# The output layer's statistics, normalisation and first transpositions move into the last chunk of the last graph layer

## The chip, the cores and the metric

The kernel runs on one core of a Trainium2 chip. Its time is the device time of one execution in microseconds; the figure for the kernel before is the median of three runs. Five engines work side by side, each with a queue of its own: TensorE (PE, with PEld for its weight loads), VectorE (DVE), ScalarE (ACT), GpSimd (POOL) and SyncE (SP), which issues most of the DMAs.

## The reference, cut to what matters

A network of four layers works on N = 2708 nodes with D = 256 features in float32. Each layer is a graph attention followed by a feed-forward part, both with a residual. Only the last layer and a helper of the third are touched:

```python
# layer 3, the last
x = x + elu(softmax(where(adj > 0, leaky_relu(f1[:, None] + f2[None, :]), NEG), axis=1) @ Wh)
#   with h = layernorm(x), Wh = h @ W, f1 = Wh @ a1, f2 = Wh @ a2
x = x + (layernorm(x) @ weight.T + bias)          # the output layer
```

The output layer needs, for each row of x, its mean and variance over the 256 features, so a row can only be normalised when the attention of that row is complete. Rows don't depend on each other in this layer.

## The kernel before, in words

The nodes are 22 tiles of 128 rows, the last one with 20 (`NT = 22`, `LAST = 21`). `X` holds all of x in SBUF, one slice `X[:, t, :]` per tile, through the whole kernel. A planner that knows the engines orders each engine's instructions when the program is built: it takes them in the order of the text where it can, and lets an engine take later ones while an earlier one waits. `issue_after(x)` keeps instructions behind x, and `manual_schedule(engines={PE})` gives TensorE the order of the text, with no moves.

The attention of one head is `gat_single` (L1301); the third graph layer runs it with the key g2 (plain residual), the fourth with g3 (`elu` true). After a projection stage it goes through the rows to be computed in chunks of `W = 6 * P` columns: three chunks of six tiles (0 to 5, 6 to 11, 12 to 17) and a last one of three (18 to 20). Tile 21, with its 20 rows, is done apart, in `tail_sums`. In each chunk, j runs over the 22 tiles of neighbours:

- `gat_pairs` (L721) makes `e`: L731 on ScalarE (an activation), L732 on VectorE (times the mask). `e` has three buffers.
- L1463 adds `e` times `V` to one accumulator `acc` per tile of the chunk. A chunk of six tiles is six matmuls per j, the last chunk three. Each float32 matmul leaves two records in the profile.

The accumulators come from a pool of eight PSUM banks. After a chunk, for each tile: L1469 `rd` (VectorE, reciprocal of the sum), L1477 `h` (ScalarE, scaled copy, which frees the bank), then the ELU and residual: L1479 `g` = min(h, 0), L1480 exp on ScalarE, L1481 `h` = max(h, 0) - 1, L1482 and L1483 additions, the last into `X`. One tile's run of L1479 to L1483 is called a unit below. `rd` has two buffers, `h` six.

`tail_sums` (L81) does tile 21 at the start of the last chunk: L87, 22 narrow matmuls into one bank; L89, a ScalarE copy `ts`; L91, one matmul that folds it into a second bank.

The output layer is `linear_ffn` (L2427), called after everything of g3 is closed. It opens its own pools (PSUM: three buffers each of `tp` and `po`), loads the weights `w` (256 KB) and the bias `b` over POOL's queue, and takes statistics in groups of four tiles (`ln_stats`, L112: L160 and L161 on VectorE, L163 a Sqrt on ScalarE, L167 a reciprocal). Exp and Sqrt need different tables of ScalarE, each change being a row `ACT_TABLE_LOAD`. Then per tile:

- L124 `f` = (X - mean) * rstd on VectorE
- L132, two transpositions on TensorE into `tp`; L2443, the copy `ft` on ScalarE
- L2444, X + b on POOL
- L139, two matmuls into `po` (four records of the profile); L2448 `o` = po + X on VectorE; L2449, the store on SP. `o` has three buffers.

Of the kernel before, what the change touches and what calls it, by code (L numbers as in the profile page):

```python
# [52 lines left out]
class Net:  # L53
# [27 lines left out]
    def tail_sums(self, pool, work, et, V):  # L81
# [8 lines left out]
        ps = pool.tile([P, D + 1], F32, name="acc")  # L90
        nc.tensor.matmul(ps[: rows(LAST)], self.quarter[:, : rows(LAST)], ts, start=True, stop=True)  # L91
        return ps
# [81 lines left out]
def cosine_gnn(net, ctx, kept, x_in):  # L174
# [7 lines left out]
    with ExitStack() as ctx:  # L182
# [101 lines left out]
        for n, (i0, iw) in enumerate(chunks(512)):  # L284
# [25 lines left out]
            if len(whole) < len(its):  # L310
                with tc.issue_after(ended.ins):
                    acc.append(net.tail_sums(ptail, work, et, F))
# [988 lines left out]
def gat_single(net, key, head, feed, elu):  # L1301
# [7 lines left out]
    with ExitStack() as ctx:  # L1309
# [120 lines left out]
        work = ctx.enter_context(tc.tile_pool(name=f"{key}work", bufs=3))  # L1430
        pacc = ctx.enter_context(tc.tile_pool(name=f"{key}acc", bufs=8, space=PSUM))
# [9 lines left out]
        nc.vector.scalar_tensor_tensor(ev, ev, 1.0, net.mask[:, :, whole:], ALU.max, ALU.mult)  # L1441
        for i0 in range(0, whole, W):
            iw = min(W, whole - i0)
            its = tiles_of(i0, iw)
            acc = [pacc.tile([P, D + 1], F32, name="acc") for _ in its]
            if i0 + iw == whole:
                acc.append(net.tail_sums(pacc, work, et, V))
            for j in range(NT):
# [12 lines left out]
                for k, i in enumerate(its):  # L1461
                    ri = rows(i)
                    nc.tensor.matmul(  # L1463
                        acc[k][:ri], e[:, k * P : k * P + ri], V[:, j, :], start=j == 0, stop=j == NT - 1
                    )
            for k, i in enumerate([*its, LAST][: len(acc)]):
                r = rows(i)
                rd = small.tile([P, 1], F32, name="rd")
                nc.vector.reciprocal(rd[:r], acc[k][:r, D : D + 1])  # L1469
                if not elu:  # L1470
# [7 lines left out]
                g = work.tile([P, D], F32, name="g")  # L1478
                nc.vector.tensor_scalar(g[:r], h[:r], 0.0, None, ALU.min)  # L1479
                nc.scalar.activation(g[:r], g[:r], AF.Exp)  # L1480
                nc.vector.tensor_scalar(h[:r], h[:r], 0.0, -1.0, ALU.max, ALU.add)  # L1481
                nc.vector.tensor_tensor(g[:r], g[:r], h[:r], ALU.add)  # L1482
                nc.vector.tensor_tensor(X[:r, i, :], X[:r, i, :], g[:r], ALU.add)  # L1483
# [924 lines left out]
def biased_gnn(net, head, route):  # L2408
# [3 lines left out]
    gat_single(net, "g2", head, results, False)  # L2412


def elu_gnn(net, kept, head, route):
# [8 lines left out]
    gat_single(net, "g3", head, results, True)  # L2424


def linear_ffn(net, out):  # L2427

    nc, tc, a, X = net.nc, net.tc, net.a, net.X
    with ExitStack() as ctx:  # L2430
        big = ctx.enter_context(tc.tile_pool(name="f3big", bufs=1))
        work = ctx.enter_context(tc.tile_pool(name="f3work", bufs=3))
        psum = ctx.enter_context(tc.tile_pool(name="f3p", bufs=3, space=PSUM))
        w = net.load_weight(big, a["f3_wT"], "w")
        b = net.load_rows(big, a["f3_b"], D, "b")
        ln = net.ln_stats()
        for t in range(NT):
            r = rows(t)
            f = work.tile([P, D], F32, name="f")
            net.normed(f, t, ln)  # L2440
            ps = net.transposed(psum, f, r)
            ft = work.tile([P, 2, P], F32, name="ft")
            nc.scalar.copy(ft[:, :, :r], ps[:, :, :r])  # L2443
            nc.gpsimd.tensor_tensor(X[:r, t, :], X[:r, t, :], b[:r], ALU.add)  # L2444
            po = psum.tile([P, D], F32, name="po")
            net.matmul_k(po[:r], ft[:, :, :r], w)
            o = work.tile([P, D], F32, name="o")
            nc.vector.tensor_tensor(o[:r], po[:r], X[:r, t, :], ALU.add)  # L2448
            nc.sync.dma_start(out[span(t), :], o[:r])  # L2449
# [148 lines left out]
```

## Time and profile before

| | |
|---|---|
| median of three runs | 2592.28 us (2589.53 to 2594.91) |
| the profiled execution | 2596.85 us, span 2595.1 us |
| TensorE busy over the span | 2422.7 us, 93% |
| VectorE, ScalarE, POOL busy | 1464.5, 1058.4, 358.2 us |
| last chunk and tail sums, 2524.60 to 2557.40: TensorE, VectorE, ScalarE busy | 32.27, 21.61, 20.23 of 32.80 us |
| output layer, 2557.40 to 2592.30: TensorE, VectorE, ScalarE, POOL busy | 29.04, 24.90, 12.20, 14.39 of 34.90 us |
| granted TensorE clock, whole span | 0.966 |

A row of the timeline gives the start in us from the span's start, the length, engine, line and operation, the tiles written and read, their size, how many instructions are merged, and in brackets how long the engine had been idle and what ended that. The windows give busy time per engine with the number of instructions, then the granted clock of TensorE (1.00 is full speed), the share of DMA and GB/s.

### The profile page before, as it was taken

How to read it: one execution, taken by the hardware profiler on the slowest of the kernel's cores; microseconds unless marked ns; L12 is line 12 of the kernel's file. 1: busy time of each engine (PE TensorE's matmuls, PEld its weight loads, DVE VectorE, ACT ScalarE, POOL GpSimd, SP SyncE). 2: the span in 40 equal slices, each digit the busy share in tenths (PEclk: the TensorE clock that was granted, in tenths of full speed). 3: DMA queues.
4: the chain of work that ended last, by engine and by line, in shares of the span. 5: the costliest groups of instructions: out<-in, count | busy, mean ns of one | idle time of the engine just before them, and what ended most of it. 6: DMA issues, size and time to landing. Idle time of an engine off the chain costs nothing. (4 is left out here: it accounts for less than half of the span.)

```text
span 2595.1 us, 32725 instructions
## 1 busy us (share of the span) xinstructions
PE 2422.7 (93%) x11708; PEld 1576.9 (61%) x11708; DVE 1464.5 (56%) x3331; ACT 1058.4 (41%) x1698; POOL 358.2 (14%) x470
## 2 busy tenths in 40 slices
PE   5899998999999999979799989999979999979998
PEld 4666765686333334458678864434447777757887
DVE  7753437746888876333544557877843222243556
ACT  3444453214877773321344333344422222234454
POOL 1000003100000001134230011222232222210002
PEclk9999999979999999989899999999989999989999
DMA  8899512000000003664220010000342222150001
GB/s 286 289 290 350 176 49 71 1 6 1 1 1 1 1 1 91 168 182 157 83 74 1 1 33 25 28 25 25 112 132 52 33 34 33 22 172 1 1 1 44
DMA packets 113178, 198.00 MB, mean 76 GB/s; under 512 B 8898, under 2 KB 72128, under 8 KB 110178
## 3 DMA queue, kind: packets, MB, share of 16 engines
q1 hardware_dynamic: 90856, 149.82, 18.1%
q0 software_dynamic: 18736, 41.56, 6.3%
q10 hardware_dynamic: 3422, 4.46, 0.6%
q8 instruction: 99, 1.62, 0.3%
q14 instruction: 65, 0.53, 0.1%
HBM read 132.97 MB, written 62.83 MB: 75 GB/s over the span
## 5 line engine op out<-in xcount | busy, mean ns | idle before, releaser
L732 DVE SCALAR_TENSOR_TENSOR e<-e,mask 128x768 f32<-128x768 f32 (+3 forms) x352 | 417.6, 1217 | 244.8 <-ACT e L731 242.3
L731 ACT ACTIVATE e<-big_p,minus_one,ratio 128x768 f32<-128x768 f32 (+3 forms) x352 | 418.6, 1226 | 284.1 <-PE acc L1463 195.0
L1463 PE MATMUL acc<-V,e 128*128 128x257 f32 x1848 | 403.6, 381 | 5.6 <-DVE e L732 5.5
L1463 PEld LDWEIGHTS acc<-V,e 128*128 128x128 f32 x1848 | 351.5, 190 | 58.0 <-issue 6.9
L2274 PE MATMUL h<-w,ft 128*128 (+1 forms) x752 | 234.8, 454 | 0.5 <-ACT ft L2256 0.5
L307 PE MATMUL acc<-F,e 128*128 128x257 f32 (+1 forms) x924 | 212.5, 383 | 3.9 <-DVE e L303 3.5
L928 PE MATMUL acc<-e,V 128*64 128x512 f32 (+1 forms) x1056 | 209.7, 550 | 1.3 <-DVE e L732 1.3
L307 PEld LDWEIGHTS acc<-F,e 128*128 128x128 f32 (+1 forms) x924 | 171.6, 189 | 56.8 <-DVE e L303 29.4
L2291 DVE TENSOR_TENSOR hh<-hh,h 128x682 f32<-128x682 f32 x47 | 40.7, 866 | 240.7 <-PE h L2274 240.7
L2274 PEld LDWEIGHTS h<-w,ft 128*128 128x128 f32 x752 | 135.8, 191 | 56.3 <-issue 1.8
L928 PEld LDWEIGHTS acc<-e,V 128*64 128x64 f32 x1056 | 73.9, 138 | 151.6 <-issue 145.9
L303 DVE TENSOR_TENSOR e<-e,mask 128x512 f32<-128x512 f32 (+2 forms) x132 | 80.5, 621 | 141.0 <-ACT e L296 139.3
L2061 ACT ACTIVATE e<-sc 128x1024 f32<-128x1024 f32 (+4 forms) x131 | 107.4, 862 | 114.6 <-PE sc L2052 90.3
L2083 DVE TENSOR_TENSOR sum<-sum,e 128x1024 f32<-128x1024 f32 (+4 forms) x131 | 136.8, 1045 | 21.3 <-PE po L2077 11.2
L296 ACT ACTIVATE e<-score 128x512 f32<-128x512 f32 (+2 forms) x132 | 69.5, 544 | 170.4 <-PE score L294 145.4
L2306 PE MATMUL po<-w,ht 114*128 (+1 forms) x564 | 129.7, 379 | 0.9 <-DVE ht L2299 0.9
L2052 PE MATMUL sc<-qt,kt 64*128 64x512 f32 (+5 forms) x568 | 121.6, 546 | 1.4 <-ACT sum L2061 0.9
L2306 PEld LDWEIGHTS po<-w,ht 114*128 114x128 f32 x564 | 106.5, 189 | 22.6 <-DVE ht L2299 8.2
L939 PE MATMUL den<-e,low 128*3 128x512 f32 (+1 forms) x1056 | 117.7, 542 | 0.0
L294 PE MATMUL score<-QK 128*128 128x512 f32 (+2 forms) x264 | 111.9, 552 | 3.4 <-ACT e L296 3.0
L2077 PE MATMUL po<-e,V 128*64 128x512 f32 (+5 forms) x524 | 107.5, 527 | 1.9 <-DVE e L2067 1.9
L1869 POOL DMA_INDIRECT dys<-y,to x47 | 73.7, 1569 | 208.1 <-ACT ft L2256 190.8
(645 smaller groups left out, 3357.7 us busy)
## 6 DMA issues: line engine op xcount, KB each, us to landing
row<-in_adj SPq DMA_DIRECT2D x21, 1354.0 KB
raw<-in_adjT SPq DMA_DIRECT2D x35, 768.0 KB
hs<-zero SPq DMA_DIRECT2D x8, 2860.0 KB
hidden<-hr SPq DMA_DIRECT2D x32, 256.0 KB
wd<-in_f_wd SPq DMA_DIRECT2D x8, 1024.0 KB
kept<-mask SPq DMA_DIRECT2D x21, 338.5 KB
mask<-kept SPq DMA_DIRECT2D x21, 338.5 KB
w<-in_d_w1T SPq DMA_DIRECT2D x8, 682.0 KB
```

What stands on the lines that cost most here:

```text
L294: nc.tensor.matmul(ps[:r, :iw], QK[:, 0, span(j)], QK[:, 1, i0 : i0 + iw], start=True, stop=True)
L307: ended = nc.tensor.matmul(acc[k], e[:r, k * P : (k + 1) * P], F[:r, j, :], start=j == 0, stop=j == NT - 1)
L731: nc.scalar.activation(v, big_p[:, i], AF.Relu, bias=net.minus_one, scale=ratio)
L732: return nc.vector.scalar_tensor_tensor(v, v, 1.0, net.mask[:, j, i], ALU.add, ALU.mult)
L928: nc.tensor.matmul(acc[n][half, :iw], V[:, j, h, :], e[n][:, k, :iw], start=j == 0, stop=j == NT - 1)
L939: nc.tensor.matmul(den[g : g + Q, :iw], low[:, j, h, Q - 1 - q : 2 * Q - 1 - q], e[n][:, k, :iw], start=False, stop=j == NT - 1 and q == Q ...
L1463: nc.tensor.matmul(acc[k][:ri], e[:, k * P : k * P + ri], V[:, j, :], start=j == 0, stop=j == NT - 1)
L2052: nc.tensor.matmul(by_pairs(ps[:r, g], m, iw)[:, :, o:], kt[b, span(j)], qt[b, :, o:iw], start=True, stop=True)
L2077: nc.tensor.matmul(by_pairs(outs[n, p][b], m, iw)[:, :, o:], V[:r, j, g, :], by_pairs(e[:r, g], m, iw)[:, :, o:], start=j == 0, stop=j == ...
L2083: nc.vector.tensor_tensor(total, total, by_heads(e[:r], m, iw)[:, :, :, o:], ALU.add)
L2274: last = nc.tensor.matmul(halves[s, n][:, q, :HALF], fts[s][:, c, :], weights.w13[n][:, es[s], c, q * HALF : (q + 1) * HALF], start=c == 0 ...
L2306: last = nc.tensor.matmul(po, ht[:KP, k, :], w2[:KP, es[s], k, :], start=k == 0, stop=k == KC - 1)
```

## The change

- `tail_sums` returns a function `added` for its last matmul, the fold. `gat_single`, for g2 as for g3, calls it after j = 2 of the last chunk; the first graph layer calls it at once.
- `linear_ffn` becomes a class `Linear`, which g3 gets as `tail`. Its pools are opened inside g3, before the pool of accumulators, and `w` and `b` loaded there. It has no PSUM pool of its own and takes banks from the accumulators' pool.
- At a chunk's end only `rd` (now six buffers) and `h` are issued. The units of a chunk follow in the next chunk, one at each odd j behind the mask.
- `Linear.step` runs behind the mask of each j: statistics of the six tiles of the chunk before, one tile at j = 4, 6, ... 14; at j = 16 the inverse root of all six by Newton's method on VectorE (`inverse_root`, 12 small instructions) in place of Sqrt; from j = 16 one normalisation per j (L124's operation) with its addition of the bias on POOL. In the last chunk also the transpositions of tiles 0 and 1, at j = 18 and 20. `f` has 18 buffers, `ft` four.
- In the last chunk of g3 and after it TensorE's order is that of the text. `Linear.finish` then goes through the tiles: for t, the transpositions of t + 2, and the matmuls, `o` and store of t. The statistics of tiles 18 to 21, with the one Sqrt that is left, come in at t = 4.

```diff
@@ tail_sums
-        ps = pool.tile([P, D + 1], F32, name="acc")
-        nc.tensor.matmul(ps[: rows(LAST)], self.quarter[:, : rows(LAST)], ts, start=True, stop=True)
-        return ps
+
+        def added():
+            ps = pool.tile([P, D + 1], F32, name="acc")
+            nc.tensor.matmul(ps[: rows(LAST)], self.quarter[:, : rows(LAST)], ts, start=True, stop=True)
+            return ps
+
+        return added
@@ gat_single
+        hs = []
+
+        def unit(i, h):
+            r = rows(i)
+            g = work.tile([P, D], F32, name="g")
+            nc.vector.tensor_scalar(g[:r], h[:r], 0.0, None, ALU.min)
+            nc.scalar.activation(g[:r], g[:r], AF.Exp)
+            nc.vector.tensor_scalar(h[:r], h[:r], 0.0, -1.0, ALU.max, ALU.add)
+            nc.vector.tensor_tensor(g[:r], g[:r], h[:r], ALU.add)
+            nc.vector.tensor_tensor(X[:r, i, :], X[:r, i, :], g[:r], ALU.add)
+
         for i0 in range(0, whole, W):
             iw = min(W, whole - i0)
             its = tiles_of(i0, iw)
+            ending = tail and i0 + iw == whole
+            if ending:
+                ctx.enter_context(tc.manual_schedule(engines={mybir.EngineType.PE}))
+            if i0 + iw == whole:
+                added = net.tail_sums(pacc, work, et, V)
             acc = [pacc.tile([P, D + 1], F32, name="acc") for _ in its]
-            if i0 + iw == whole:
-                acc.append(net.tail_sums(pacc, work, et, V))
             for j in range(NT):
...
+                if j == 2 and i0 + iw == whole:
+                    acc.append(added())
+                if tail:
+                    with tc.issue_after(masked.ins):
+                        if hs and j % 2:
+                            unit(*hs.pop(0))
+                        tail.step(its[0], j, ending, pacc)
             for k, i in enumerate([*its, LAST][: len(acc)]):
                 r = rows(i)
-                rd = small.tile([P, 1], F32, name="rd")
+                rd = small.tile([P, 1], F32, name="rd", bufs=6)
...
                 nc.scalar.activation(h[:r], acc[k][:r, :D], AF.Copy, scale=rd[:r])
-                g = work.tile([P, D], F32, name="g")
...
+                hs.append((i, h))
+            while ending and hs:
+                unit(*hs.pop(0))
+            if ending:
+                tail.finish(pacc)
@@ in place of linear_ffn
+class Linear:
...
+    def norm(self, t):
+        r, X = rows(t), self.net.X
+        self.fs[t] = self.work.tile([P, D], F32, name="f", bufs=18)
+        self.net.normed(self.fs[t], t, (self.ln.mean, self.ln.rstd))
+        self.net.nc.gpsimd.tensor_tensor(X[:r, t, :], X[:r, t, :], self.b[:r], ALU.add)
+
+    def step(self, t0, j, ending, psum):
+
+        k, m = divmod(j - 4, 2)
+        if t0 and m == 0 and 0 <= k < 6:
+            self.ln.sums(t0 - 6 + k, t0 - 5 + k, root=False)
+        if t0 and j == 16:
+            self.ln.newton(self.work, t0 - 6, t0)
+            self.known = t0
+        if len(self.fs) < self.known:
+            self.norm(len(self.fs))
+        if ending and j in (NT - 4, NT - 2):
+            self.turned(len(self.fts), psum)
+
+    def turned(self, t, psum):
+        net, r, f = self.net, rows(t), self.fs[t]
+        ps = psum.tile([P, D + 1], F32, name="acc")[:, :D].rearrange("p (c m) -> p c m", c=2)
+        for c in range(2):
+            net.nc.tensor.transpose(ps[:, c, :r], f[:r, c * P : (c + 1) * P], net.ident[:r, :r])
+        ft = self.fts[t] = self.work.tile([P, 2, P], F32, name="ft", bufs=4)
+        net.nc.scalar.copy(ft[:, :, :r], ps[:, :, :r])
+
+    def result(self, t, psum):
+        net, nc, r = self.net, self.net.nc, rows(t)
+        po = psum.tile([P, D + 1], F32, name="acc")[:, :D]
+        net.matmul_k(po[:r], self.fts[t][:, :, :r], self.w)
+        o = self.work.tile([P, D], F32, name="o")
+        nc.vector.tensor_tensor(o[:r], po[:r], net.X[:r, t, :], ALU.add)
+        nc.sync.dma_start(self.out[span(t), :], o[:r])
+
+    def finish(self, psum):
+
+        early = self.known
         for t in range(NT):
-            net.normed(f, t, ln)
-            ps = net.transposed(psum, f, r)
...
+            if t == 4:
+                self.ln.sums(early, NT)
+                self.ln.roots(early, NT)
+            if t + 2 < NT:
+                if t + 2 not in self.fs:
+                    self.norm(t + 2)
+                self.turned(t + 2, psum)
+            self.result(t, psum)
```

## The prediction

> **What bounds the kernel now.** I read the page first, for the bound of the whole: TensorE is busy 93% of the span, and the chain that ended last closes with the output layer's matmuls.
>
> ```profile
> span 2595.1 us, 32725 instructions
> PE 2422.7 (93%) x11708; PEld 1576.9 (61%) x11708; DVE 1464.5 (56%) x3331; ACT 1058.4 (41%) x1698; POOL 358.2 (14%) x470
> ...
> PE po L139 1%; PE tp L132 0%; ACT ft L2443 0%; DVE f L124 0%; DVE o L2448 0%; ACT h L1477 0%; ACTq L2443 0%; DVE rstd L167 0%; DVEq L2448 0%
> ```
>
> Then the timeline of TensorE over the last 80 us, which is where the diff works. Columns: start, length, engine and line, count, and in brackets the idle time before and what ended it.
>
> ```profile
> 2524.64 2.79 PE L87 MATMUL acc<-V,et 128*32 128x257 f32 x44
> 2527.96 0.61 PE L91 MATMUL acc<-ts,quarter 128*20 128x257 f32 x2 [0.53 <-ACT ts L89]
> 2528.50 28.90 PE L1463 MATMUL acc<-V,e 128*128 128x257 f32 x132
> 2560.48 1.54 PE L132 MATMUL tp<-ident,f 128*128 128x128 f32 x6 [3.08 <-ACT h L1477]
> 2561.82 5.04 PE L139 MATMUL po<-w,ft 128*128 128x256 f32 x12
> 2567.86 0.41 PE L132 MATMUL tp<-ident,f 128*128 128x128 f32 x2 [1.00 <-DVE f L124]
> 2568.81 0.41 PE L132 MATMUL tp<-ident,f 128*128 128x128 f32 x2 [0.54 <-DVE f L124]
> 2569.05 1.89 PE L139 MATMUL po<-w,ft 128*128 128x256 f32 x8
> ...
> 2574.38 0.82 PE L132 MATMUL tp<-ident,f 128*128 128x128 f32 x6
> 2575.28 2.86 PE L139 MATMUL po<-w,ft 128*128 128x256 f32 x12
> ...
> 2589.64 2.10 PE L139 MATMUL po<-w,ft 128*128 128x256 f32 x8 [0.29 <-ACT ft L2443]
> ```
>
> The last chunk is solid TensorE work until 2557.40. The output layer then takes 34.44 us, until the last o starts on VectorE at 2591.84, with four kinds of loss: 3.08 us before the first transposition (its PSUM banks belong to a pool that opens when the last h copy has released the old one), 1.00 and 0.54 us for f (rows 2567.86, 2568.81), a wait for ft after every three tiles, and a slow first group (x12 takes 5.04 us; later ones 2.86). The last is the clock: the same stretch cut in windows, with the granted clock in the third column from the end.
>
> ```profile
> 2556.10:2559.50 3.40, 1.30 (x6) 0.78 (x5) 1.96 (x10) 2.70 (x5) 1.51 (x3) 1.00 0.00 0
> 2559.50:2562.90 3.40, 2.42 (x9) 2.11 (x10) 3.02 (x11) 2.48 (x9) 0.00 (x0) 0.50 0.00 0
> 2562.90:2566.30 3.40, 3.40 (x10) 2.69 (x9) 2.93 (x12) 1.65 (x3) 0.00 (x0) 0.50 0.11 39
> ```
>
> TensorE was busy 1.30 of 3.40 us, and the next 6.8 us ran at half clock. The Trainium skill (TensorE: Matmul & The Clock Gate, Part 1) has the gate close after an idle window of about 3.4 us; here 3.08 us sufficed, so I treat a busy share, not a full idle window, as the trigger.
>
> **The output layer after its move.** The built order shows TensorE's queue after the last accumulation as tp(t+2), po(t) for t = 0 to 19, then po(20), po(21): 20 pairs of transpositions and 22 pairs of matmuls. Two pairs of transpositions went into the chunk, behind j = 18 and j = 20. Prices: a po tile is four records; the x8 row starts at 2569.05 and its successor at 2570.78, so 0.216 each, 0.864 per tile. Six transpositions take 0.82 us of which 0.27 is the last one's latency: 0.109 each, 0.218 per tile. If nothing waits, 22 x 0.864 + 20 x 0.218 = 23.4 us, plus 0.1 to VectorE: the last o starts 23.5 us after the last accumulation, instead of 34.44. Gain 10.9 us. It is made of the 3.08 us, about 3 us of half clock, 1.9 us of waits for f, some 2.4 us of waits for ft, and 0.44 us of transpositions put in the chunk.
>
> Does anything wait? Walked by hand over the three queues from the last accumulation (T = 0):
> - Of the eight banks, tp(2) and po(0) get ones that are free long before, tp(4) and po(2) those of tiles 18 and 19, whose h copies end by 0.5 us; later a bank is free once its ft or o has been read out.
> - ScalarE does h(18), h(19), one exp, h(20), h(21), one exp, and only then ft(2): at 0.36 to 0.47 us each it ends near 2.3 us, and po(2) is due at 2.4. This is the tightest place; I put 0.1 us of wait inside the stall below. Then ft(3) ends at 3.0, due 3.5, and the margin grows to over 1 us.
> - VectorE does the last four tiles' units, then o(0) at about 4.1 us, and has caught up with the matmuls by o(7). The one Sqrt table load (1.28 us on ScalarE) falls after ft(8), and ft(9) still ends 1 us before it is due; f(18) is ready near 9.6 us, and its transposition is due at 17.7.
> - Output: in the trace's DMA packets the first o, begun at 2564.14, had landed by 2565.90, 1.76 us. With three o buffers that permits one tile in 0.6 us; TensorE gives one in 1.08.
>
> **The fold of the tail sums.** L91 waited for the ScalarE copy ts: from the end of L87 (2527.43) to the first accumulation (2528.50) is 1.07 us, of which L91 itself needs 0.43. After the change nine accumulations stand between, so 0.64 us is gained. The third graph layer has the same edit and the same row (L87 ends at 1488.96, accumulations begin at 1489.98): 0.59 us. Copies h issued ahead of all units at a chunk's end take away a 0.34 us pause at 2412 where a bank waited for an h: 0.3. Together 1.5 us.
>
> **What the last chunk pays.** Four transpositions: 0.44 us of TensorE. Statistics, Newton's inverse root and normalisation of tiles 0 to 11 go into earlier chunks with 2.6 us per j, of which VectorE uses 0.96: hidden. In the last chunk a j has 1.30 us. VectorE issues: mask 0.48; a unit 0.20 + 0.20 + 0.34 + 0.34 = 1.07 on odd j from 1 to 11; statistics 0.42 on even j from 4 to 14. So two j cost 0.95 + 1.07 + 0.42 = 2.44 of 2.60 us: hidden with little to spare. With three e buffers, e(j) can be masked 1.14 us before it is needed, and this is the cover. From j = 16 it doesn't reach. Newton is 12 small dependent operations (0.164 each in the table of groups, 0.22 with the hand-over): 2.7 us. Then come five normalisations before the last mask, and each starts a bias addition on POOL, which shows here:
>
> ```profile
> 1322.91 2.88 DVE L732 SCALAR_TENSOR_TENSOR e<-e,mask 128x768 f32<-128x768 f32 x2
> ...
> 1341.67 0.96 DVE L732 SCALAR_TENSOR_TENSOR e<-e,mask 128x768 f32<-128x768 f32 x1 [1.26 <-ACT e L731]
> ...
> 2567.31 0.40 DVE L124 TENSOR_SCALAR f<-X,mv,rstd 128x256 f32<-128x256 f32 x1
> 2567.76 2.69 DVE L124 TENSOR_SCALAR f<-X,mv,rstd 128x256 f32<-128x256 f32 x4
> ```
>
> The first row lies under POOL's additions of a bias in the third layer, the second after them: a mask is stretched from 0.96 to 1.4 us. A normalisation goes from 0.33 us per issue to 0.73. By these rows: 2.7 + 0.33 + 4 x 0.73 + 5 masks x 0.48 + 3 x 0.26 of stretch = 9.1 us, against 5 x 1.30 + 0.44 + 1.14 = 8.1 us: TensorE waits 1.0 us. The skill speaks harder against the change: SBUF — State Buffer, "Who interferes with whom", has whoever comes second blocked for the whole of the other's instruction. Then each of five normalisations or masks loses a POOL addition of 0.77 us: 2.7 + 5 x 0.33 + 2.4 + 5 x 0.77 = 10.6, and TensorE waits 2.5 us. I take the rows, 1.0 us; the ends are 0 (no contention: 6.75 us) and 2.5. Behind a late mask, in the fixed TensorE order, stand the transpositions and everything else of TensorE.
>
> POOL and SP issue the same instructions in the same order as before: weights (256 KB) and bias go out behind the mask's flags at the start of the layer, and POOL stands idle 245.21 us before the first addition. The weights now wait for the projection stage's buffers; only the bias and the additions queue behind them. No cost.
>
> **Sum.** 10.9 + 1.5 - 0.44 - 1.0 = 11.0 us. The profiled execution took 2596.85 us, 1.75 more than its span, and becomes 2585.9. It lies 4.6 us above the median of the runs; on the median 2592.28 the same 11.0 us gives 2581.3 us, 0.42% faster. The runs before spread from 2589.53 to 2594.91, so about 0.2%, 5.2 us, is what a measurement tells from no change.
>
> **Rivals.**
> - The last chunk stalls enough to lose the clock. The 2.5 us wait of the harsher reading leaves a 3.4 us window poorly filled, and 6.8 us at half clock follow (as above): 1.5 + 3.4 us less gain, 6.1 us, 2586.2 us. For it: the stretched rows and 0.73 us of measured stretch per normalisation; against: by the rows the excess is 1 us, under a third of a window.
> - Writing out is the bound. The steady groups before wrote three tiles in 3.59 us. If that is already the rate of the writes (1.2 us a tile), 22 tiles take 26.3, 2.9 us less gain: 2584.2 us. Against it: 1.76 us of landing with three buffers, and higher rates elsewhere on the page.
> - The lookahead fails, and it gets slower. Each po waits for its own ft: transposition 0.22, latency 0.16, copy 0.37, two hand-overs 0.1, matmuls 0.864 with 0.1 for an unprefetched weight load, 1.81 us a tile, 39.9 for 22. The loss against 34.44 is 5.4 us, and 1.0 + 0.44 - 1.5 leaves it there: 2597.6 us. It decides from (34.44 - 23.5) / 22 = 0.50 us of wait in each tile. For it: a wait for ft after each group before, and a fixed order that lets nothing pass. Against: ft has four buffers, and each transposition stands two tiles ahead.
> - It doesn't do what it says, because the end of the kernel is set elsewhere. The chain ends in po and o, so this needs a bound I don't see: 2592 us.
>
> **How the numbers follow.** Main 0.70; lost clock 0.17; writes 0.05; lookahead failing 0.04; no effect 0.04. The first three are faster by over 0.2%: 0.92, less 0.01 for a lost clock that costs more; same 0.05; slower 0.04. The range: below, no stall (1.0) and 2 us for the spread of a median, 2578; above, the lost clock's 2586.2 and 1.3 for the spread, 2587.5. What lies beyond is the last two cases and some of the second.
>
> **What would show it.** The first L132 transposition outside the chunk within 0.3 us of the last accumulation; no half clock between there and the end; one po tile in about 1.08 us, and some 23.5 us from the last accumulation to the last o; no wait for ts before the fold; masks from j = 17 on the ones TensorE waits for, about 1 us in all. The prediction is wrong if po waits for ft in each tile, if o waits for a DMA, or if masks from j = 3 to 15 come late.

## The result, and the profile after

| | before | after |
|---|---|---|
| median of 12 runs each | 2593.37 us (2589.53 to 2599.89) | 2583.55 us (2577.48 to 2589.30) |
| ratio, with its 95% interval | | 0.9956 [0.9946, 0.9967] |
| the profiled execution, its span | 2596.85, 2595.1 us | 2585.36, 2583.2 us |
| last accumulation to the start of the last o | 34.44 us | 23.81 us |
| first L87 to the end of the last accumulation | 32.76 us | 33.22 us |

The kernel is faster by 0.44%; the interval means 8.6 to 14.0 us. The prediction said 2581.3 us, 11.0 us less than before; the medians differ by 9.8 us, the spans by 11.9.

The page of the kernel after gives these busy times. Over the span TensorE has as many instructions as before and 2 us less busy time.

```profile
PE 2420.7 (94%) x11708; PEld 1575.7 (61%) x11708; DVE 1472.5 (57%) x3362; ACT 1050.1 (41%) x1687; POOL 360.8 (14%) x470
```

The timeline of TensorE for the same stretch, columns as before (in the code after the change L1483 is the accumulation, L93 the fold, L2492 the transposition, L143 the output matmuls):

```profile
2523.24 2.79 PE L87 MATMUL acc<-V,et 128*32 128x257 f32 x44
2525.97 4.17 PE L1483 MATMUL acc<-V,e 128*128 128x257 f32 x18
2530.07 0.61 PE L93 MATMUL acc<-ts,quarter 128*20 128x257 f32 x2
2530.61 21.09 PE L1483 MATMUL acc<-V,e 128*128 128x257 f32 x96
2551.54 0.38 PE L2492 MATMUL acc<-ident,f 128*128 128x128 f32 x2
2552.06 2.87 PE L1483 MATMUL acc<-V,e 128*128 128x257 f32 x12
2554.77 0.38 PE L2492 MATMUL acc<-ident,f 128*128 128x128 f32 x2
2554.99 1.47 PE L1483 MATMUL acc<-V,e 128*128 128x257 f32 x6
2556.29 0.38 PE L2492 MATMUL acc<-ident,f 128*128 128x128 f32 x2
2556.51 1.03 PE L143 MATMUL acc<-w,ft 128*128 128x256 f32 x4
2557.37 0.38 PE L2492 MATMUL acc<-ident,f 128*128 128x128 f32 x2
2557.59 1.03 PE L143 MATMUL acc<-w,ft 128*128 128x256 f32 x4
2558.46 0.38 PE L2492 MATMUL acc<-ident,f 128*128 128x128 f32 x2
...
2576.02 1.03 PE L143 MATMUL acc<-w,ft 128*128 128x256 f32 x4
2576.98 0.30 PE L2492 MATMUL acc<-ident,f 20*128 20x20 f32 x2
```

The accumulations end at 2554.99 + 1.47 = 2556.46, and the third transposition pair is already in the array: no pause, no bracket until the end, one tile in 1.08 us (2557.37 to 2558.46). From the last accumulation to the last o TensorE is busy 23.71 of 23.81 us; before it was 29.04 of 34.44. So half of the gain there is idle time, and half is shorter work, more than half of that the half clock, at which the kernel before did 2.42 + 3.40 us of work. VectorE's last row closes it at 2580.27, which gives the 23.81 us:

```profile
2580.27 0.41 DVE L2501 TENSOR_TENSOR o<-acc,X 20x256 f32<-20x256 f32 x1 [0.55 <-PE acc L143]
```

The window over the seam shows TensorE full and the clock at 1.00 where the kernel before had 1.30 us of work in a window and 0.50 after it:

```profile
2556.10:2559.50 3.40, 3.40 (x20) 2.91 (x19) 3.29 (x15) 3.20 (x10) 0.00 (x0) 1.00 0.00 0
```

One thing in the first timeline doesn't fit the prediction's sizes: between the transpositions at 2551.54 and the accumulation at 2552.06 lie 0.52 us where the pair itself takes 0.22. That is the stall of the last chunk, 0.30 us. VectorE there:

```profile
2549.55 1.47 DVE L128 TENSOR_SCALAR f<-X,mv,rstd 128x256 f32<-128x256 f32 x3
2550.93 1.08 DVE L736 SCALAR_TENSOR_TENSOR e<-e,mask 128x384 f32<-128x384 f32 x1
2551.93 0.81 DVE L128 TENSOR_SCALAR f<-X,mv,rstd 128x256 f32<-128x256 f32 x1
2552.67 0.55 DVE L736 SCALAR_TENSOR_TENSOR e<-e,mask 128x384 f32<-128x384 f32 x1
```

The mask of j = 19 is twice as long as its successor and ends at 2552.01, and TensorE goes on at 2552.06. POOL was adding the bias beside it:

```profile
2550.04 2.56 POOL L2473 TENSOR_TENSOR X<-X,b 128x256 f32<-128x256 f32 x3 [31.34 <-DVE f L128]
2552.82 0.97 POOL L2473 TENSOR_TENSOR X<-X,b 128x256 f32<-128x256 f32 x1 [0.23 <-DVE f L128]
```

### The profile page after: what moved, and what is told of

Its sections match the earlier page's. It is cut to its first block, busy times and chain, and to the rows that moved or that the text cites. A ratio compares the mean times of both kernels' runs of the same rounds, so it can differ in the third digit from the quotient of the medians.

```text
span 2583.2 us, 32667 instructions
## 1 busy us (share of the span) xinstructions
PE 2420.7 (94%) x11708; PEld 1575.7 (61%) x11708; DVE 1472.5 (57%) x3362; ACT 1050.1 (41%) x1687; POOL 360.8 (14%) x470
## 4 chain that ended last, share of the span: by engine, by line
PE 41%; DVE 5%; DMA 3%; ACT 1%; issue 1%; POOL 0%; SPq 0%; DVEq 0%; POOLq 0%; ACTq 0%
PE acc L1483 14%; PE h L2300 8%; PE po L2332 4%; PE sc L2078 3%; PE po L2103 3%; PE pv L143 2%; PE pj L2049 2%; DVE sum L2109 2%; DMA dys<-y,to 2%; PE pt L2324 1%; DVE yt L2122 1%; PE acc L143 1%; PE s1p L1378 1%; PE wy L143 1%; DVE e L736 1%
## 5 line engine op out<-in xcount | busy, mean ns | idle before, releaser
L1483 PE MATMUL acc<-V,e 128*128 128x257 f32 x1848 | 402.6, 380 | 5.7 <-DVE e L736 5.5
L1483 PEld LDWEIGHTS acc<-V,e 128*128 128x128 f32 x1848 | 350.3, 190 | 57.8 <-issue 6.5
```

What stands on the lines that cost most here:

```text
L1483: nc.tensor.matmul(acc[k][:ri], e[:, k * P : k * P + ri], V[:, j, :], start=j == 0, stop=j == NT - 1)
```

## The experiments

The theory: the output layer is a chain TensorE, ScalarE, TensorE whose two links are hidden by transposing two tiles ahead; the pause at the seam is a matter of PSUM banks and costs its own length and some 3 us of half clock; the last chunk pays with a small stall. Rivals: the pause costs only itself; VectorE and POOL block each other fully; the order by hand is what counts. In the kernels below line numbers are their own. "Tail" is the time from the last accumulation to the start of the last o, "chunk" that from the first L87 to the end of the last accumulation.

### Lookahead taken out

```diff
-        if ending and j in (NT - 4, NT - 2):
-            self.turned(len(self.fts), psum)
...
-            if t + 2 < NT:
-                if t + 2 not in self.fs:
-                    self.norm(t + 2)
-                self.turned(t + 2, psum)
+            if t + 2 < NT and t + 2 not in self.fs:
+                self.norm(t + 2)
+            self.turned(t, psum)
             self.result(t, psum)
```

> The changed kernel with the transpositions of tile t directly ahead of its matmuls, none in the last chunk; TensorE order still fixed. The measure is the tail, from the end of the last accumulation to the start of the last o: 34.44 us before, 23.81 us changed. My theory (the lookahead is what makes po follow po; without it each po waits for its own ft): 1.81 us a tile at full clock, a tail of about 40 us, 5 us slower than the kernel before and 16 us slower than the changed one; more if the pauses cost the clock. Rival (the gain is the early statistics and the gapless switch, the order matters little): a tail of at most 27 us.

Ratio to before 1.0027 [1.0015, 1.0038]: 7.0 us slower. Tail 41.94 us, chunk 32.99. TensorE's timeline:

```profile
2555.13 0.38 PE L2490 MATMUL acc<-ident,f 128*128 128x128 f32 x2
2557.24 1.13 PE L143 MATMUL acc<-w,ft 128*128 128x256 f32 x4 [1.73 <-ACT ft L2492]
2559.05 1.13 PE L143 MATMUL acc<-w,ft 128*128 128x256 f32 x4 [0.46 <-ACT ft L2492]
```

This edit also takes the two early pairs out of the chunk. Each tile waits for its own copy ft and takes 1.81 us (2557.24 to 2559.05), later 1.87. This is the prediction's slower rival, made to happen at the price that it was given (1.81 us a tile; its tail was put at 39.9 us, and the 1.73 us wait of the first tile and the 1.87 make the rest). Early statistics and shared banks without the lookahead lose 7.0 us.

### The lookahead alone, on the kernel before

```diff
+        ctx.enter_context(tc.manual_schedule(engines={mybir.EngineType.PE}))
...
+        turned(0)
+        turned(1)
+        for t in range(NT):
+            r = rows(t)
+            if t + 2 < NT:
+                turned(t + 2)
+            ft = fts[t]
```

(`turned` holds the old loop's lines for f, tp, ft and the bias; the pools f3work and f3p get four buffers instead of three.)

> The kernel before with this part alone: in its output layer the transpositions stand two tiles ahead, four buffers in place of three, TensorE order fixed there; own PSUM pool, statistics and switch as before. My theory (four losses that add up): only the waits for ft go, 2.4 us; the tail is 32 us instead of 34.44, the 3.08 us pause, the half clock and the waits for f stay. Rival (lookahead is nearly all of it): a tail of 25 us.

Ratio 0.9987 [0.9979, 0.9996], tail 30.88 us: 3.56 us less than before. The timeline has lost the waits for ft but keeps the other two losses:

```profile
2564.88 0.87 PE L132 MATMUL tp<-ident,f 128*128 128x128 f32 x6 [3.42 <-ACT h L1477]
...
2570.50 0.41 PE L132 MATMUL tp<-ident,f 128*128 128x128 f32 x2 [1.05 <-DVE f L124]
```

Half clock lasted 3.4 us here, with 2.88 us of work in it, and 6.8 before, with 2.42 + 3.40: half of the difference in work, some 1.5 us of the 3.56, is owed to the clock, and why it fell less is no merit of the order (see the doses below). The order of the matmuls by itself, with its fourth buffers, is worth some 2 us of the tail. The remaining 7.07 us of the 10.63 in the tail need what stands before the seam: the bank free at once and the clock kept with it, f ready, two pairs transposed early.

### The output layer in banks of its own

```diff
-        pacc = ctx.enter_context(tc.tile_pool(name=f"{key}acc", bufs=8, space=PSUM))
+        cacc = ctx.enter_context(ExitStack())
+        pacc = cacc.enter_context(tc.tile_pool(name=f"{key}acc", bufs=8, space=PSUM))
...
-                tail.finish(pacc)
+                cacc.close()
+                tail.finish(ctx.enter_context(tc.tile_pool(name="f3p", bufs=8, space=PSUM)))
```

> The changed kernel, but the output layer takes its banks from a pool of its own that opens when the accumulators' pool is closed. Then the first transposition behind the last accumulation waits for the copy h of tile 21, which ended 1.3 us after the last accumulation. My theory: a pause of 1.3 to 1.6 us, no drop of the clock for so short a pause, a tail of about 25.2 us. Rival (any pause at the switch brings the half clock): 1.5 us and 3.4 us more, a tail of 28.7 us.

Ratio 0.9962 [0.9950, 0.9974], tail 25.41 us, 1.60 more than with the rotation kept. The pause is back, and the clock stays at 1.00:

```profile
2556.67 0.44 PE L2494 MATMUL acc<-ident,f 128*128 128x128 f32 x2 [1.39 <-ACT h L1505]
```

So there is a pause as soon as the first bank stands behind the last h, as the prediction read it. But the pool explains 1.39 us, not the 3.08 of the kernel before. There ScalarE changed its table between the first two copies h and the last two (L1477), because a Sqrt for statistics (at 2537.33) had come since its last exp:

```profile
2557.70 1.28 ACT L1480 ACT_TABLE_LOAD   x1
2558.99 0.72 ACT L1480 ACTIVATE g<-g 128x256 f32<-128x256 f32 x2
2559.62 0.81 ACT L1477 ACTIVATE h<-acc,rd 128x256 f32<-128x256 f32 x2
```

In the changed kernel and in this one Newton's root stands in place of that Sqrt, so no table is loaded in the last chunk or at its end, and one exp instead of two stands ahead of the last two copies. The load alone is 1.28 of the 1.69 us between the two pauses. So the change shortens the seam in two ways, and Newton's root is one of them; no run here puts the load back by itself. A pause of 1.39 us drew no half clock; the next two kernels make it longer.

### Doses of a pause

```diff
+            if ending:
+                tail.delay(hs[0][1], 3)
             while ending and hs:
                 unit(*hs.pop(0))
...
+    def delay(self, h, n):
+        nc, f = self.net.nc, self.fs[2]
+        zero = self.work.tile([P, D], F32, name="zero", bufs=1)
+        nc.vector.tensor_scalar(zero, h, 0.0, None, ALU.mult)
+        for _ in range(n):
+            nc.gpsimd.tensor_tensor(f, f, zero, ALU.add)
```

The second kernel has 6 in place of 3. Each was executed once; what follows is read from the traces.

> The changed kernel with TensorE made to wait at the seam and nothing else changed: f of tile 2, whose transposition is the first TensorE work after the last accumulation, gets three POOL additions of a tile of zeros made from h of tile 18 (the output stays the same). The pause is estimated at 2.7 us (h copy 0.4, one VectorE operation and a hand-over 0.3, three additions between 0.6 and 0.8). Theory (a 3.4 us window that TensorE fills for less than about half is followed by half clock, as the 3.08 us pause of the kernel before was): the granted clock goes to 0.50 for one or two windows, and from the last accumulation to the last o it takes 23.8 + 2.7 + 1.7 to 3.4 = 28.2 to 29.9 us. Rival (only a window of 3.4 us without any work closes the gate, and the half clock of the kernel before came from its later waits for f): clock stays at 1.00, 26.5 us.

> The same with six additions: pause about 4.9 us. Theory: half clock for two windows (6.8 us, 3.4 us lost), 23.8 + 4.9 + 3.4 = 32.1 us from the last accumulation to the last o. Rival (a window wholly without work is needed): a pause of 4.9 us covers a whole window only if it starts within 1.5 us of a window's end, so more likely than not the clock stays at 1.00 and it takes 28.7 us.

Three additions: a pause of 2.83 us, a tail of 29.82 us, so 6.01 us more than without, of which 3.18 are not the pause. Its first row after the seam, and windows set on the change of the clock (columns: length, busy time of PE, PEld, DVE, ACT, POOL, then the clock):

```profile
2559.00 0.69 PE L2501 MATMUL acc<-ident,f 128*128 128x128 f32 x2 [2.83 <-POOL f L2495]
```

```profile
2554.81:2558.22 3.41, 1.36 (x7) 0.85 (x5) 2.57 (x10) 2.71 (x7) 2.37 (x4) 1.00 0.00 0
2558.22:2561.63 3.41, 2.63 (x9) 2.17 (x10) 3.41 (x12) 0.69 (x2) 0.72 (x1) 0.50 0.00 0
2561.63:2565.03 3.40, 3.40 (x11) 2.66 (x11) 1.46 (x4) 1.05 (x3) 0.00 (x0) 0.50 0.14 47
```

Six additions: the pause is 6.03 us (4.9 was estimated; the six took 5.72 us), the tail 32.70 us, of which 2.86 us are lost to half clock. The windows:

```profile
2555.23:2558.63 3.40, 2.16 (x11) 1.52 (x10) 2.56 (x10) 2.11 (x6) 2.34 (x4) 1.00 0.00 0
2558.63:2562.03 3.40, 0.00 (x0) 0.00 (x0) 3.40 (x7) 1.02 (x3) 3.17 (x4) 1.00 0.00 0
2562.03:2565.44 3.41, 2.03 (x6) 1.71 (x7) 2.34 (x6) 0.68 (x2) 1.25 (x2) 0.50 0.00 0
2565.44:2568.85 3.41, 3.41 (x11) 2.67 (x10) 1.55 (x5) 0.74 (x2) 0.00 (x0) 0.50 0.11 38
```

The same for the lookahead alone, whose pause of 3.42 us fell over the border of two windows:

```profile
2559.75:2563.16 3.41, 1.71 (x8) 1.14 (x6) 2.93 (x10) 1.91 (x3) 2.63 (x4) 1.00 0.00 0
2563.16:2566.57 3.41, 1.55 (x9) 1.26 (x10) 2.84 (x11) 2.75 (x9) 0.00 (x0) 1.00 0.00 0
2566.57:2569.98 3.41, 2.88 (x9) 1.72 (x7) 3.32 (x14) 2.35 (x5) 0.00 (x0) 0.50 0.11 38
```

Where the windows are cut is not a choice of the reader. In each trace here the changes of the clock lie on one grid of 3.413 us: in the kernel before 34 changes, all within 0.03 us of it. But the grid lies elsewhere in each execution. Counted from the start of the span, its first line is at 2.92 us in the kernel before, at 1.81 in the changed kernel, at 1.64, 2.01 and 3.19 with three additions, with six and with the lookahead alone. Where a pause falls on it is luck.

Put together:

| kernel | pause at the seam | TensorE busy in the last window ahead of half clock | half clock | tail |
|---|---|---|---|---|
| after | 0 | none: no half clock | 0 | 23.81 |
| own banks | 1.39 | none: no half clock | 0 | 25.41 |
| three additions | 2.83 | 1.36 of 3.41 | 6.8 us | 29.82 |
| before | 3.08 | 1.30 of 3.40 | 6.8 us | 34.44 |
| lookahead alone | 3.42, later 1.05 | 1.55 of 3.41 (the one before, 1.71, drew none) | 3.4 us | 30.88 |
| six additions | 6.03 | 0.00 of 3.40 (the one before, 2.16, drew none) | 6.8 us | 32.70 |

A wholly empty window isn't needed: 1.36 us of work in the window didn't prevent half clock, and the 2.83 us pause contained no empty window. The rival in which the gate needs one falls. At this seam a window filled for 1.55 us or less is followed by half clock, one filled for 1.71 or more is not. Over all thirteen traces, cut along their grids and without the first 30 us of the program, each of the 124 windows at full clock with under 1.4 us of TensorE work was followed by half clock; between 1.4 and 2.0 us some were and some were not. Busy time doesn't say it all: in a few stages with narrower matmuls (8 rows or 1 row by 128 among them) half clock also follows windows with more, in the kernel before one with 3.03 us.

```profile
542.20:545.60 3.40, 3.03 (x30) 2.77 (x29) 0.78 (x2) 0.54 (x2) 0.00 (x0) 1.00 0.00 0
545.60:549.00 3.40, 2.30 (x24) 2.09 (x22) 1.27 (x3) 1.17 (x2) 0.00 (x0) 0.51 0.00 0
```

So the same pause can cost different amounts. The 3.42 us of the lookahead alone were cut in two by a line of the grid. By these figures, an estimate, a pause of 3.08 us leaves a window with under 1.4 us of work at about three of four positions on the grid, and one of 1.39 us at none. The 3 us that the kernel before lost to half clock are a reading of one execution; how often it loses them, no run here shows.

### Statistics of the last six early tiles left to the output layer

```diff
-        if t0 and m == 0 and 0 <= k < 6:
+        late = t0 == LAST - LAST % 6
+        if t0 and not late and m == 0 and 0 <= k < 6:
...
-        if t0 and j == 16:
+        if t0 and not late and j == 16:
```

> The changed kernel with statistics, inverse root and normalisation of tiles 12 to 17 not in the last chunk but at the end, with those of tiles 18 to 21. My theory (the last chunk pays for them a little, and the end has room): the pause of 0.3 us ahead of the mask at j = 19 goes; f(12) is due 10.9 us after the last accumulation and VectorE has it at 10 to 12 us, so 0 to 1.5 us of wait: tail 23.8 to 25.3 us, the whole within 1 us of the changed kernel. Rival (early statistics carry a large part of the gain): 2 us or more of waits for f and a tail of 26 us or more.

Ratio 0.9956 [0.9933, 0.9980], chunk 32.80 us, tail 23.81 us. Without Newton, normalisations and bias additions in the last chunk the stall is gone, and the transpositions follow each other without a gap:

```profile
2549.61 0.38 PE L2493 MATMUL acc<-ident,f 128*128 128x128 f32 x2
2549.83 2.77 PE L1483 MATMUL acc<-V,e 128*128 128x257 f32 x12
```

Two things follow. What the last chunk pays for its statistics is 33.22 - 32.80 = 0.42 us (0.30 in the pause, most of the rest in the next twelve accumulations, 2.87 against 2.77 us). And the statistics of tiles 12 to 17 needn't be there: the tail is as short without them, since VectorE has them ready in time. 0.42 us is too little for the times to show, so this is no faster version by any measurement here.

### Bias additions moved out of the chunks, twice

```diff
-        self.net.nc.gpsimd.tensor_tensor(X[:r, t, :], X[:r, t, :], self.b[:r], ALU.add)
...
+            r, X = rows(t), self.net.X
+            self.net.nc.gpsimd.tensor_tensor(X[:r, t, :], X[:r, t, :], self.b[:r], ALU.add)
             self.result(t, psum)
```

> The changed kernel, but POOL adds the output bias to X(t) only in the output layer, just ahead of o(t), instead of behind each normalisation in the chunks. Theory (what the last chunk waits, 0.3 us, is stretch of masks and normalisations under POOL's additions): in the last chunk, normalisations at 0.4 us and masks at 0.56, no wait for a mask, 0.3 us less from the first L87 to the last accumulation (32.9 instead of 33.22); the output layer stays at 23.8 us, since an addition of 0.4 to 0.8 us fits under 1.08 us a tile. Time ratio as for the changed kernel, 0.9956. Rival 1 (the pause is owed to the length of VectorE's own queue, Newton's chain above all): the pause of 0.3 us stays. Rival 2 (o now waits for POOL): 22 tiles at more than 1.08 us, up to 1.5 if o and the additions block each other; up to 9 us lost, ratio 0.999.

Ratio 0.9959 [0.9945, 0.9972], chunk 33.22 us, tail 23.81 us: the trace is that of the changed kernel. The edit moved nothing. POOL's row stands where it stood, with the line of its new place, 31.35 us after POOL's last work:

```profile
2556.27 2.56 POOL L2515 TENSOR_TENSOR X<-X,b 128x256 f32<-128x256 f32 x3 [31.35 <-DVE f L128]
```

POOL has nothing else in its queue, so an addition that comes later in the text still starts when its f has been read. The run is silent on both its theories; only a real dependence puts work off:

```diff
-        self.net.nc.gpsimd.tensor_tensor(X[:r, t, :], X[:r, t, :], self.b[:r], ALU.add)
+        if not 12 <= t < 18:
+            self.net.nc.gpsimd.tensor_tensor(X[:r, t, :], X[:r, t, :], self.b[:r], ALU.add)
...
                 self.ln.roots(early, NT)
+                self.norm(18)
+                b, X = self.work.tile([P, D], F32, name="blate", bufs=1), self.net.X
+                self.net.nc.vector.scalar_tensor_tensor(b, self.fs[18], 0.0, self.b, ALU.mult, ALU.add)
+                for i in range(12, 18):
+                    self.net.nc.gpsimd.tensor_tensor(X[:, i, :], X[:, i, :], b, ALU.add)
```

> The changed kernel, with the six bias additions of the last chunk (tiles 12 to 17) really put off: they add a copy of the bias that is made from f of tile 18, which is normalised only in the output layer (the earlier attempt to put them off left them behind their normalisations, since POOL's queue is empty there). Statistics, Newton and the six normalisations stay in the chunk. Theory (the 0.30 us pause is the one stretched mask and the stretched normalisations, together about 0.5 + 2 x 0.4 us that VectorE pays ahead of the mask of j = 19): normalisations at 0.40, the mask of j = 19 at 0.56, no wait for a mask, 32.80 us from the first L87 to the last accumulation instead of 33.22. Rival (VectorE's own queue is too long, Newton plus three normalisations in a row): the pause of 0.3 us stays, 33.2 us. The output layer 23.8 us by both; ratio 0.996 by both, 0.4 us being too little for a time to show.

Ratio 0.9961 [0.9947, 0.9974], chunk 32.80 us, tail 23.81 us. VectorE in the last chunk:

```profile
2552.48 1.06 DVE L128 TENSOR_SCALAR f<-X,mv,rstd 128x256 f32<-128x256 f32 x3
2553.45 0.55 DVE L736 SCALAR_TENSOR_TENSOR e<-e,mask 128x384 f32<-128x384 f32 x1
2553.92 0.41 DVE L128 TENSOR_SCALAR f<-X,mv,rstd 128x256 f32<-128x256 f32 x1
```

Three normalisations take 1.06 instead of 1.47 us, one takes 0.41 instead of 0.81, the mask of j = 19 takes 0.55 instead of 1.08, and the pause is gone. Newton and the normalisations alone fit under the cover; the 0.42 us are POOL's additions and nothing else.

### POOL's load doubled

```diff
-        self.net.nc.gpsimd.tensor_tensor(X[:r, t, :], X[:r, t, :], self.b[:r], ALU.add)
+        for _ in range(1 + (12 <= t < 18)):
+            self.net.nc.gpsimd.tensor_tensor(X[:r, t, :], X[:r, t, :], self.b[:r], ALU.add)
```

> The changed kernel with POOL's load in the second half of the last chunk doubled: for tiles 12 to 17 the bias is added twice (these tiles' output is too large by one bias; the work of all other engines is the same). Theory (VectorE and POOL only stretch each other, as the rows of the kernel before show: a normalisation 0.33 to 0.73 us an issue, a mask 0.48 to 0.74): POOL is now at work through all of the normalisations and the masks between, some 2 to 3 operations more are stretched by 0.26 to 0.4 us, the wait in the chunk grows from 0.3 to 0.6 to 1.5 us. Rival (full blocking: whoever comes second waits for the whole of the other's instruction): six more additions of 0.77 to 0.97 us are each paid in full by VectorE, of which five stand ahead of the last mask, so the wait grows by about 4 us to 4.2 us, and a window of 3.4 us falls short of work, so that half clock may follow.

Ratio 0.9961 [0.9948, 0.9974]. Chunk 33.33 us, only 0.11 more, but tail 25.62 us, 1.81 more. Neither reading in the expectation had looked at the tail. POOL's row of twelve additions runs 10.64 us, past the last accumulation, and stretches the units of the last tiles. VectorE and then ScalarE and TensorE behind the seam:

```profile
2560.01 0.77 DVE L1453 TENSOR_SCALAR g<-h 128x256 f32<-128x256 f32 x1
...
2563.57 0.81 DVE L1453 TENSOR_SCALAR g<-h 128x256 f32<-128x256 f32 x1
```

```profile
2564.41 0.42 ACT L1454 ACTIVATE g<-g 128x256 f32<-128x256 f32 x1 [1.92 <-DVE g L1453]
2564.74 0.63 ACT L2495 COPY ft<-acc 128x256 f32<-128x256 f32 x2
```

```profile
2565.14 1.13 PE L143 MATMUL acc<-w,ft 128*128 128x256 f32 x4 [1.25 <-ACT ft L2495]
```

g of a unit takes 0.77 to 0.81 us where it is 0.28 alone, the exp of that unit waits for it, and behind the exp in ScalarE's queue stands the copy ft that TensorE needs. Six more additions cost 0.11 + 1.81 = 1.92 us, 0.32 each. The rival's full price was about 4 us of wait in the chunk. It falls: in the middle of POOL's row one normalisation, one mask and two additions take 1.74 us together (two normalisations begin at 2554.96 and 2556.70), where one after the other they would take 0.33 + 0.47 + 2 x 0.73 = 2.26. The two engines slow each other but overlap in part. An operation of VectorE that meets an addition pays 0.40 (f), 0.53 (mask) or 0.49 to 0.53 us (g), about half of the addition's 0.73 to 0.97.

### The fold put back

```diff
             acc = [pacc.tile([P, D + 1], F32, name="acc") for _ in its]
+            if i0 + iw == whole:
+                acc.append(added())
...
-                if j == 2 and i0 + iw == whole:
-                    acc.append(added())
```

> The changed kernel with the fold of the tail sums put back: the matmul of the fold is issued at once behind the tail sums, in both graph layers, instead of after j = 2. By the prediction the fold cost 0.64 us in the fourth layer and 0.59 in the third, so TensorE would wait that much for ts in each, and the span grows by 1.2 us. By the trace of the changed kernel, where changes between narrow and wide matmuls left gaps of about 0.1 us on both sides of the moved fold, the move is worth 0.40 us a layer: from the first L87 to the last accumulation 33.22 + 0.40 = 33.6 us in the fourth layer. Rival (the later fold only moved the wait, since something else holds TensorE there): no difference. The output layer stays at 23.8 us; ratio 0.9959 to 0.9961 against 0.9956.

Ratio 0.9956 [0.9943, 0.9968]; tail 23.81 us; chunk 33.56 us, so 0.34 us more, and 32.71 against 32.37 us for the same stretch of the third graph layer.

```profile
2528.21 0.61 PE L93 MATMUL acc<-ts,quarter 128*20 128x257 f32 x2 [0.47 <-ACT ts L89]
2528.75 24.99 PE L1485 MATMUL acc<-V,e 128*128 128x257 f32 x114
```

The wait for ts is what the move removes, as predicted, and each layer is paid 0.34 us for it, not 0.64 and 0.59.

### Without the order by hand

```diff
-            if ending:
-                ctx.enter_context(tc.manual_schedule(engines={mybir.EngineType.PE}))
```

> The changed kernel without the order fixed by hand for TensorE in the last chunk: the planner places TensorE's instructions as it does elsewhere. Theory (the gain is in the banks and in the lookahead, and the order by hand only writes down what the planner would choose too): the same rows, transposition and po tile in 1.08 us, 23.8 us from the last accumulation to the last o, 33.2 us from the first L87 to the last accumulation. Rival (the planner pulls transpositions ahead of accumulations or po behind several transpositions): other rows in the output layer, waits for ft after groups of three tiles as in the kernel before, 26 us or more.

One execution: chunk 33.21 us, tail 23.81 us, the same rows in the same order. The order by hand changes nothing here; the lookahead is in the order of the text.

## Why the prediction was right

The gain came from where it was looked for. By the profiled executions:

| term of the sum | predicted | measured | by |
|---|---|---|---|
| output layer's tail | 10.9 (34.44 to 23.5) | 10.63 (to 23.81) | traces before and after |
| fold, fourth and third layer | 0.64 + 0.59 | 0.34 + 0.34 | the fold put back |
| pause at the chunk boundary | 0.3 | 0.35 | first accumulation of the fourth layer to the first L87: 172.21 and 171.86 us, neither with half clock in it |
| transpositions in the chunk | -0.44 | -0.44 | two pairs of 0.22 each |
| stall from j = 17 on | -1.0 | -0.42 | bias additions put off |
| sum | 11.0 | 10.8 | |

That the sum comes so near is luck in part: the fold brought 0.55 us less than was put down for it, and the stall took 0.58 less, and the two cancel. The spans differ by 11.9 us, 1.1 more than this sum. Chance is in that: up to the first L87 the third graph layer's chunks took 173.54 us before and 171.86 after, because a window of half clock fell into them before. With POOL's load doubled they took 173.54 too.

- **The tail** had all its parts. The transposition starts behind the last accumulation without a pause, no half clock, 1.08 us a tile, no wait for ft. Two of the losses it removes were taken as fixed, and are not: of the 3.08 us, 1.28 were the table load, which the prediction's reading of the pool leaves out, and the half clock depends on where the pause falls on the grid. The 0.31 us over 23.5 are three changes between full and narrow matmuls at the tile of 20 rows, not in the step: from the po row at 2576.02 to its successor are 0.96 us where it is 0.87 elsewhere (2557.59 to 2558.46), and two more such steps follow. The tightest place, the copy ft of tile 2, ended at 2558.34, and po of tile 2 began at 2558.67: a margin of 0.3 us where 0.1 was put.
- **The fold** was the term that was over-sized. The step took 1.07 us less 0.43 for L91 as gain. But L91 held TensorE for 0.54 us, before (2527.96 to 2528.50) as after (2530.07 to 2530.61), so only the wait of 0.53 could be gained. And the moved fold stands between full matmuls, which makes two more changes of shape: the 18 accumulation records ahead of it take 4.10 us where 18 at 0.218 are 3.92. 0.53 less 0.18 is 0.35. Each change between narrow weights (20 or 32 columns) and full ones leaves about 0.1 us.
- **The stall** was over-sized too, and its rival reading more so. Newton's twelve operations took 0.18 us each with the hand-over (2546.45 to 2549.55, less two masks of 0.47, is 2.16), not 0.22; and of the five masks only one was stretched, by 0.53, since from then on VectorE came first and POOL's addition waited (0.97 instead of 0.73). Of the normalisations the first two, begun before POOL's first addition, took 0.41, and the others were stretched as the row had said, to 0.81. With these sizes the prediction's sum is 7.9 us against its 8.1, no wait at the last mask; the 0.30 us came earlier, at the mask of j = 19, which a sum closed at the last mask doesn't look at. So a wait of the foretold kind came, but not where the sum looks for it. That POOL is the cause, the two runs with the additions put off and doubled show. For the harsher rule, full blocking and 2.5 us, 0.42 was measured.
- **The rivals.** Lost clock: the stall wasn't large enough, 0.14 us of idle time in a stretch of a window's length (3.27 of 3.41 busy between 2549.29 and 2552.70). Writes: one o in the tail did wait for a DMA, 1.1 us, which the prediction had named as a sign of being wrong; TensorE was not held, so the bound of the rival isn't there. No mask from j = 3 to 15 came late: the 96 accumulation records from 2530.61 to the transpositions at 2551.54 follow each other at 0.218 us. Lookahead failing: didn't happen; forced, it cost what it was said to cost a tile. No effect: excluded by the interval.
- **Against the medians** 9.8 was measured, and the interval of 8.6 to 14.0 holds the 11.0 predicted. The level was off by 2.25 us, of which 1.09 are the median before, that is 2593.37 over twelve runs and was 2592.28 over three.

What stays open: executions of one kernel spread over some 12 us (2577.48 to 2589.30) while tail and chunk stay the same from trace to trace (span 2583.2 us for the changed kernel, 2589.4 with the bias moved in the text, tail and chunk alike). The clock's windows are part of it, as in the third layer; the rest was not followed. The medians of the kernel before beside the experiments (2593.55, 2597.63 and 2597.37 us, on three chips) differ by more than most of the edits do, so the small terms above rest on the traces alone, each on one execution of each kernel. What in TensorE's work, beside its busy time, the clock goes by is open too.

## What to carry to other kernels

Where one engine needs another's result for each tile (transpose, copy, multiply), put the first step of tile t + 2 ahead of the last step of tile t: here that is the difference between 1.08 and 1.81 us a tile, and it pays in full only if the first of these steps are already done when the stage begins, from the same banks. A pause of TensorE at a seam between stages is to be priced with the clock, and the clock's part is a matter of chance: 1.39 us cost 1.6, 2.83 us cost 6.0 in the one execution that was seen. Look on the other engines for what makes the pause long: here a table load of 1.28 us on ScalarE. When work is put under another engine's cover, look at what runs beside it: the additions on the idle POOL were the only thing in the last chunk that TensorE felt, and twice as many were paid one stage later, through ScalarE's queue.

## What was not expected of the hardware

- Half clock follows a pause before any 3.4 us window is empty: a window with 1.36 of 3.41 us of TensorE work was followed by 6.8 us at 0.50, one with 1.55 by 3.4 us; one with 1.71 was not. Elsewhere in the program one with 3.03 us of work was. The windows lie on a grid of 3.413 us that stands elsewhere in each execution, so the same pause is not always followed by the same loss.
- An operation of VectorE that meets a POOL addition of 0.73 to 0.97 us is longer by 0.40 to 0.53 us, whether it has one or two tensors to read (f 0.41 to 0.81, mask 0.55 to 1.08, g 0.28 to 0.81). When POOL comes second, it is POOL that gets longer and VectorE pays nothing (masks of 0.55 beside additions of 0.97). Neither waits for the whole of the other: two additions, a normalisation and a mask take 1.74 us, not 2.26.
- A change between matmuls with 20 or 32 columns of weights and full ones costs TensorE about 0.1 us; two of them took a third of what the fold had to gain. Transpositions and output matmuls, both with full weights, alternate without such a loss (0.22 + 0.87 us a tile).
